# Fifty-seven passes without a use in TensorE's list, at eight places of the opening and the end

## The chip, the cores and the metric

The kernel runs on one core of one Trainium2 chip. The time is device microseconds from start to end of one execution; of the kernel before, three executions are shown by their median. One further execution was taken by the hardware profiler, and all rows below are of that one. The engines are PE (TensorE; PEld are its weight loads), DVE (VectorE), ACT (ScalarE), POOL (GpSimd) and SP (SyncE), each with its own list of instructions that it works off in order.

## The reference

For 32 batches of `x` (512 channels by 1024 nodes) a graph attention layer and a graph convolution follow each other, each with a residual and a layer norm over the last axis:

```python
q = einsum('c,bcn->bn', wq, x);  k = einsum('c,bcn->bn', wk, x)
scores = q[:, None, :] + k[:, :, None]
att = softmax(where(scores > 0, scores, 0.01 * scores), axis=-1)
agg = einsum('bcn,bmn->bcm', x, att)
x = layernorm(x + relu(einsum('oc,bcm->bom', adj, agg) + bm[None, :, None]))
W = adj * adj
x = layernorm(x + einsum('bnf,nm->bmf', x, W) + bias)
```

## The kernel before

The softmax over a sum `q + k` is not computed as a 1024 by 1024 matrix. Each batch goes through these steps, which carry short names in the order that the code writes out by hand:

- `p0` to `p27` (`project`, L329): the product of the transposed `adj` with `x`, in a form with seven instead of eight block products, into PSUM tiles `zp_A`, `zp_B`, `zp_C`. `k...` (`keep`, L348 on DVE or L350 on ACT) read them into `zrow`; `x...` (`mix`, L318) make the operands' sums.
- `qb` and `mx` (L367, L374): transposes that spread `q` and its largest value; `mx` needs `pk` (L355, DVE), and `mr` reads it.
- `r...` (`place`, L394, DVE) count each node's rank, `sd...` (`send`, L406, POOL) scatter the rows by rank to a table in DRAM, `fe` (`fetch`, L452 and L457) brings the sorted rows back as `zs`.
- `wx` (L467, ACT) and `wb` (L479, L487, DVE) make the weights `lq`; `t0` to `t8` (`table`, L501, PE) form prefix and suffix sums block by block, into a PSUM tile `tp`; `e0` to `e8` (`table_out`, L513, ACT) copy it out, `cp` (POOL) and `ca` (ACT), both L519, carry one row on to the next blocks; `ts` stores them. So t(k+1) needs e(k), then cp(k) and ca(k).
- `c...` (L419, ACT) count signs, `pi...` (`pick`, L534, POOL) gather three rows for each node. `oa`, `ox`, `no` (L549 to L566) make the mixing weights, `sc` (L573, ACT) and `ga`, `gb` (L578, DVE) mix the rows.
- `u0` to `u3` (`turn`, L587, PE) transpose the mixed rows; `ad` (L594, DVE) adds `x`; `sq` (L603), `rt` (POOL) and `y0` to `y3` (L619, ACT) are the first norm.
- `sA`, `sB` (`seed`, L649) put the bias into PSUM by two bf16 products each; `T1` to `T4` (`less`, L643, DVE) form operand differences; `m0` to `m13` (`multiply`, L666) are the second layer in seven block products, into `oA`, `oB`, `oC`. One f32 product of the program is two rows of the trace. `rd...` (L687 DVE, L689 ACT) read them, and `st`, `ro`, `sf`, `av`, `so` are the last norm and the store.

PSUM is given out by four tags, `A`, `B`, `C` and `T`, of one tile of 128 by 1024 f32 each. `bank(tag, ...)` takes the tag's tile anew, and the first write of a new tile waits until the reads of the one before are done. `T` serves `qb` of most batches and `t0` to `t7`; `t8`, `mx` and `u` use `C` in most batches.

No scheduler orders the work. `BEGIN`, `SLOT` and `END` are lists of step names, and each engine runs its instructions in the order in which the steps stand there. `BEGIN` interleaves the first batches by hand (`@b` names the batch from there on), `SLOT` is one round of the steady part, run with four batches in flight, and `END` is the drain of batches 28 to 31. The tile `first` (bf16, 128 by 1920), made once at the start, holds the smallest normal number in one corner and zeros elsewhere; `r...` uses it as a mask.

Of the kernel before, what the change touches and what calls it, by code (L numbers as in the profile page):

```python
# [23 lines left out]
def gat_gcn_resnorm_kernel(  # L24
# [823 lines left out]
    qw2 p25 @1 x04 @0 p24 k112 k011 k122 qb p26 ql p27 r0 p13 k121 r1 p12 k111 r2 en pk sd1 r3 mx @1
    p2 @0 sd0 r4 @1 p5 @0 sd3 r5 @1 p3 @0 mr sd4 r6 @1 p4 p0 @0 sd5 r7 @1 k0p1 p1 @0 sd2 @1 p7 k011
    p6 @0 sd6 @1 x14 @2 x01 @1 p12 k0u2 @0 sd7 sb0 @1 p13 p10 k0p5 p8 p9 x13 p11 k012 @2 x02 @1 p16  # L850
    @0 fe @1 k022 p17 @0 sb1 @1 p14 k1p5 p15 @0 sb2 @1 p21 k021 p19 @0 c0 @1 p18 p20 k1p1 @0 c1 @1
    k111 p22 p23 @0 wx0 wb0 t0 @2 x11 @1 k1u2 @2 x12 @1 p25 @2 x03 @0 e0 @1 p24 k112 @0 ca0 ts0 cp0
    c2 t1 @1 k122 @0 wx1 @1 qb @0 wb1 e1 @1 p27 @0 ts1 @1 ql @0 cp1 @1 pk @0 c3 @1 p26 r0 @2 p4 @1
    k121 r1 @0 c4 @1 en @0 ca1 t2 @1 r4 @0 c5 @1 sd1 r5 @2 p5 @0 e2 ca2 @1 mx @0 ts2 cp2 @1 mr @0 c6
    @1 sd4 @0 t3 @1 r2 @2 p2 @1 sd0 r3 @0 e3 ca3 ts3 cp3 @1 r6 @0 t4 @2 p1 @1 sd5 r7 @0 e4 ca4 cp4
    @1 sd3 @0 t5 @2 p3 @1 sd7 @0 e5 ts5 @2 k0p1 @0 cp5 ca5 @1 sd2 @0 t6 @2 p0 @0 e6 @2 k0p5 @0 cp6
    ts6 @2 k011 @0 ca6 @1 sd6 @0 t7 @2 x13 x14 p6 @0 e7 @2 p7 @0 ca7 cp7 ts7 t8 ts4 @2 k0u2 p11 @0
    e8 c7 @2 p10 @0 ts8 @1 fe @0 sh @2 k022 x04 p14 @0 qw3 pi0 @2 p15 p9 @1 wx0 wb0 @2 k021 @1 c0 @2
    p18 @1 t0 c1 @2 p19 @1 c2 @2 p8 @1 e0 ca0 cp0 ts0 @2 k012 @1 c3 @0 pi2 @2 k1p1 @0 pi1 @2 p22 @0
    pi3 @2 p23 @0 pi7 @2 p17 @0 pi5 @2 k1u2 p16 @1 c4 @0 pi6 @1 t1 @2 k1p5 @1 wx1 @0 pi4 @2 p24 @1  # L860
    wb1 c5 @2 p20 p12 p25 p21 p13 @0 oa0 ox0 sx no0 @2 k122 @0 sc0 @2 k112 @1 e1 @2 p27 @0 ga0 sc2
    @1 ts1 ca1 cp1 @0 sc1 gb0 @1 t2 @0 ga1 gb1 @1 e2 @0 sc3 @2 k111 @1 cp2 ca2 @0 ga2 @1 t3 @0 ga3
    gb3 @2 p26 @0 oa1 @1 e3 @0 ox1 @1 cp3 @0 no1 gb2 sc4 sc5 ga4 sc6 ga5 @1 ca3 @0 ga6 sc7 @1 t4 @0
    gb5 @1 c6 @0 ga7 gb4 gb7 @1 e4 @0 gb6 u0 @1 ca4 ts4 @2 k121 @1 cp4 ts3 c7 @0 ad0 @1 t5 ts2 @0 u1
    @1 sh e5 @0 sq0 u2 @1 cp5 @0 ad1 @1 ca5 t6 @0 rt0 @3 ld0 @2 en @0 ad2 sq1 @2 pk @0 u3 @1 e6 @3
    ld1 @2 mx @1 ca6 cp6 @0 sB @2 mr @0 sq2 rt1 ad3 @1 t7 @0 qw5 @3 ld2 @1 e7 @0 sA @1 ts6 @0 rt2 y0
    @2 qb @1 ts5 cp7 ca7 @2 r0 @1 ts7 t8 @0 sq3 @2 r1 @1 e8 @0 rt3 y1 m1 @1 ts8 @2 r2 sd1 @3 ld3 @2
    ql r3 sd0 @0 y2 m0 @2 r4 sd2 @0 y3 m7 qw4 @2 c0 @1 pi3 @0 T1 m6 @2 c1 r5 @1 pi2 @0 rdp1 m2 @1
    pi1 @0 T2 @2 c2 r6 @1 pi0 @0 m5 @2 c3 @0 T3 m4 T4 @3 x01 @0 m3 @2 r7 @0 rdu2 rd11 m9 @2 sd7 @0
    rdp5 @1 sx @2 c4 sd5 @0 m8 @1 pi5 @0 m11 rd22 @2 sd4 @0 m10 @1 pi6 oa0 ox0 @2 c5 @1 no0 @2 sd3  # L870
    @0 m13 @3 x02 @1 sc2 @3 x03 @1 sc1 @2 sd6 @0 rd12 @1 sc0 @0 m12 @3 x04 @1 pi7 @0 rd21 @1 pi4 @2
# [15 lines left out]
    r2 sd1 @29 sq3 @31 r3 sd0 @29 y1 m0 @30 pi3 @31 r4 c0 @30 pi2 @31 r5 @29 m1 @30 pi0 @29 T1 rt3
    @31 r6 @29 m2 rt2 @31 r7 sd2 @29 y2 m3 @31 sd3 @30 sx @29 rdp5 @30 pi1 @29 y3 m11 @31 sd5 @29
    rdp1 T2 @31 c1 sd7 @29 m5 @31 c2 sd6 @29 m7 @31 c3 sd4 @29 m10 @30 pi7 pi5 @29 m6 @30 oa0 ox0
    no0 @29 m4 T3 @30 sc3 sc0 @29 rd11 @31 fe @29 rdu2 T4 @31 c4 @29 m9 @30 sc2 @31 c5 @29 m8 @31 c6  # L890
    @29 rd22 @30 sc1 @31 c7 @29 rd12 m13 st0 @31 wx0 wb0 t0 @30 ga3 ga0 ga1 @31 e0 ca0 @29 st1 @31
    ts0 cp0 @30 pi6 @31 t1 @30 gb1 @29 m12 @31 e1 @30 gb3 @31 ca1 ts1 cp1 wx1 @29 ro0 @31 wb1 @29
    rd21 @31 t2 @30 pi4 ga2 @29 sf0 st2 @31 e2 ca2 cp2 t3 e3 ca3 cp3 @29 av0 ro1 @31 t4 @29 sf1 @30
    gb0 @31 e4 cp4 @30 oa1 ox1 @31 ca4 t5 @30 no1 gb2 sc4 sc5 ga4 sc7 ga5 @31 e5 @30 ga7 sc6 @31 cp5
    ca5 @30 ga6 @31 t6 @29 av1 @30 gb4 gb6 @29 so1 @30 gb5 @31 e6 @30 gb7 u1 @31 ca6 ts6 @29 st3 @31
    cp6 @29 ro2 @31 ts4 t7 ts2 @30 u0 @31 e7 ts3 ca7 @30 u3 @31 cp7 ts7 t8 @30 ad0 @31 ts5 e8 @30
    ad1 sq0 @31 ts8 @30 u2 @29 sf2 @31 sh @29 so0 @30 sq1 rt0 ad2 @31 sx @30 ad3 sq2 @31 pi0 @30 sA
    y0 rt1 @31 pi1 @30 y1 m1 @31 pi3 @30 sq3 T1 @31 pi2 @30 m0 rt2 sB rdp1 rt3 m3 y2 @31 pi7 @30 y3
    m7 @31 pi5 @30 T2 m6 @31 pi4 @30 T4 @31 pi6 @30 T3 m4 @29 ro3 @31 oa0 @30 m5 @31 ox0 no0 @30
    rd11 @31 sc2 @30 m2 rdu2 @31 ga2 sc3 @30 m9 @31 gb2 sc1 sc0 ga1 @30 rdp5 m8 @31 ga3 ga0 @29 av2  # L900
    @31 gb3 @30 m11 rd22 @31 gb0 @30 m13 @31 oa1 ox1 no1 @30 m12 @31 gb1 sc4 sc7 ga4 @30 m10 @31 sc5
    ga7 @30 rd21 @31 gb4 gb7 sc6 ga5 ga6 gb5 gb6 u0 @30 rd12 @31 u1 ad0 u2 sq0 ad1 u3 ad2 sq1 rt0
    ad3 sB y0 rt1 @30 st0 @31 sA y1 m0 @29 sf3 @31 sq2 @30 ro0 @31 T1 m1 sq3 rt2 m3 y2 rt3 y3 m2
    rdp1 T2 m6 rdp5 @30 st1 @29 av3 @31 m5 @30 sf0 st2 ro1 @31 m4 T4 @30 ro2 @31 T3 m7 rdu2 @30 sf1
    @31 rh110 @30 av1 st3 @31 m8 @30 so1 sf2 @29 so2 @30 ro3 av2 @29 so3 @31 m9 rh220 @30 av0 @31
    rh111 hb21 m10 rh221 @30 sf3 @31 hb31 @30 av3 @31 m11 rh120 @30 so3 @31 st0 @30 so0 so2 @31 m12
# [59 lines left out]
```

## Time and profile before

| | |
|---|---|
| median of three executions | 2204.18 us (2203.93 to 2204.54) |
| the profiled execution | 2203.48 us, of which the span from first to last instruction is 2201.8 us |
| mean granted TensorE clock | 0.989 |
| PE busy | 2109.1 us (96%) |
| DVE, ACT, POOL busy | 1776.1, 1653.9, 986.5 us |
| PE's longest waits in all | tp for POOL's copy, 16.6 us in 23 times; oA for ACT's y, 5.9 us in 5 times |

A row of the timeline has its start (us from the span's start), its length, the engine, the line, what is written from what, the shape, the number of instructions merged, and in brackets the idle time of that engine just ahead of it with what ended it. The busy time by stretches gives each engine's busy time in a stretch of the span, and the granted clock: 1.00 is the full clock, 0.50 half of it. Ends of PE's rows are modelled: a row outlasts the start of the next one where they are pipelined.

### The profile page before, as it was taken

To read this page: it belongs to the slowest core of one execution; us is meant where nothing else is said; L and a number is where in the kernel's file an instruction comes from. 1 tells how busy PE (TensorE), PEld (TensorE's weight loads), DVE (VectorE), ACT (ScalarE), POOL (GpSimd) and SP (SyncE) were. 2 spreads that over 40 slices of the span, in tenths; PEclk is the share of its full clock that TensorE was granted. 3 is DMA by queue.
4 is the path that set the end of the run, shared out by engine and by line. 5 is a ranking of instruction groups with operands and counts; after the bars stand their busy time and mean duration, and the time that the engine had idled before them with its cause. 6 is when DMAs were issued, how large, how long until landed. Compare 5 with 4: busy or idle time off the path is not lost.

```text
span 2201.8 us, 35460 instructions
## 1 busy us (share of the span) xinstructions
PE 2109.1 (96%) x11697; PEld 1235.6 (56%) x11697; DVE 1776.1 (81%) x3576; ACT 1653.9 (75%) x2758; POOL 986.5 (45%) x1291
## 2 busy tenths in 40 slices
...
PEclk9989999999999999999999999999999999999998
...
GB/s 249 162 224 255 263 272 280 260 236 244 263 257 280 251 240 256 262 260 280 259 244 239 270 255 282 264 244 245 263 256 279 278 247 238 260 264 270 220 206 96
DMA packets 178768, 548.84 MB, mean 249 GB/s; under 512 B 27020, under 2 KB 27032, under 8 KB 178584
## 3 DMA queue, kind: packets, MB, share of 16 engines
...
q14 instruction: 91, 0.75, 0.1%
q10 hardware_dynamic: 24, 0.01, 0.0%
...
## 4 chain that ended last, share of the span: by engine, by line
PE 73%; ACT 8%; DMA 5%; issue 4%; DVE 4%; POOL 4%; SPq 1%; POOLq 0%; DVEq 0%; ACTq 0%
PE zp_A L329 17%; PE oA L666 15%; PE tp L501 12%; PE zp_B L329 7%; PE oB L666 7%; PE op L587 5%; PE zp_C L329 4%; PE oC L666 4%; DMA zs<-td 3%; ACT rows L573 1%; ACT y L619 1%; DMA td<-zrow,ranki 1%; ACT v L689 1%; POOL zs L519 1%; PE qb L367 1%
## 5 line engine op out<-in xcount | busy, mean ns | idle before, releaser
L578 DVE SCALAR_TENSOR_TENSOR rows<-rows,ra 128x512 f32<-128x512 f32 x512 | 365.7, 738 | 19.5 <-ACT rows L573 15.7
L501 PE MATMUL tp<-zs,lq 128*64 128x257 f32 x2304 | 338.3, 394 | 27.3 <-POOL zs L519 16.6
L406 POOL DMA_INDIRECT td<-zrow,ranki x256 | 268.3, 1048 | 213.7 <-DVE idx L430 80.2
L666 PE MATMUL oA<-y,adj_sb 128*128 128x512 f32 x768 | 352.2, 601 | 9.8 <-ACT y L619 5.9
L534 POOL DMA_INDIRECT rows<-td,idx x256 | 297.2, 1161 | 90.2 <-issue 68.7
L394 DVE SCALAR_TENSOR_TENSOR junk<-qb,zrow,first 128x1024 int8<-128x1024 f32 x240 | 307.0, 1279 | 10.9 <-PE qb L367 4.0
L519 POOL COPY zs<-ts 1x513 f32<-1x513 f32 x128 | 92.0, 719 | 477.9 <-ACT ts L513 477.7
L329 PE MATMUL zp_A<-wb,x 128*64 128x257 f32 (+1 forms) x1536 | 280.3, 388 | 13.9 <-ACT v L689 6.5
L419 ACT ACTIVATE junk<-lq,kc 128x1024 int8<-128x1024 f32 x240 | 274.5, 1144 | 2.0
L594 DVE SCALAR_TENSOR_TENSOR y<-op,nbm,x 128x1024 f32<-128x1024 f32 x128 | 163.8, 1282 | 128.8 <-PE op L587 128.6
L666 PEld LDWEIGHTS oA<-y,adj_sb 128*128 128x128 f32 x768 | 146.5, 192 | 189.0 <-issue 139.5
L501 PEld LDWEIGHTS tp<-zs,lq 128*64 128x64 f32 x2304 | 171.1, 137 | 135.1 <-POOL zs L519 37.0
L573 ACT ACTIVATE rows<-rows,ra 128x512 f32<-128x512 f32 x256 | 180.0, 718 | 80.0 <-DVE ra L566 78.4
L329 PEld LDWEIGHTS zp_A<-wb,x 128*64 128x64 f32 (+1 forms) x1536 | 178.6, 155 | 77.4 <-ACT v L689 17.8
L350 ACT COPY zrow<-zp_A 128x514 f32<-128x514 f32 x192 | 112.7, 587 | 143.6 <-PE zp_A L329 129.8
L519 POOL COPY zs<-zs 1x513 f32<-1x513 f32 x128 | 79.0, 617 | 253.3 <-ACT zs L513 253.3
L619 ACT ACTIVATE y<-y,nb,r 128x1024 f32<-128x1024 f32 x128 | 158.8, 1241 | 4.3
L695 DVE BATCH_NORM_STATS2 st<-v 128x6 f32<-128x512 f32 x240 | 151.8, 674 | 0.0
L603 ACT ACTIVATE x<-y,nm 128x1024 f32<-128x1024 f32 x128 | 147.2, 1150 | 4.2
L719 ACT ACTIVATE v<-v,nb,rs 128x1024 f32<-128x1024 f32 x120 | 148.1, 1234 | 2.3 <-DVE nb L711 1.4
L587 PE MATMUL op<-ident,rows 128*128 128x128 f32 x1024 | 141.5, 283 | 4.2 <-DVE rows L578 2.0
L587 PEld LDWEIGHTS op<-ident,rows 128*128 128x128 f32 x1024 | 114.9, 143 | 46.0 <-issue 24.6
...
## 6 DMA issues: line engine op xcount, KB each, us to landing
x<-in_x_dram SPq DMA_DIRECT2D x128, 512.0 KB, 4.5
out_dram<-v SPq DMA_DIRECT2D x120, 512.0 KB, 2.9
...
td<-ts SPq DMA_DIRECT2D x224, 120.2 KB, 2.0
...
```

Source lines behind the costliest of these rows:

```text
L329: nc.tensor.matmul(zp[n : n + wide, m, 0:CE], side(b, g, a)[:, c, m * P + n : m * P + n + wide], wb[:, w, c, :], start=first and c == 0, s ...
L394: nc.vector.scalar_tensor_tensor(junk(b)[:, 0:N], qbs[b], zrow[:, nt, 0:1], first[:, o : o + N], ALU.subtract, ALU.is_lt, accum_out=rank[: ...
L406: sc = nc.gpsimd.indirect_dma_start(out=td[:, :], out_offset=bass.IndirectOffsetOnAxis(ap=ranki[:, nt : nt + 1], axis=0), in_=zrow[:, nt, ...
L419: nc.scalar.activation(junk(b)[:, N : 2 * N], qs[b], AF.Sign, bias=kcs[b][:, nt : nt + 1], accum_out=signs(b)[:, nt : nt + 1],)
L501: nc.tensor.matmul(tp[i * G : (i + 1) * G, h, 0:CE], lw[:, ks[i], :], zs[:, j, 1 + h * CE : 1 + (h + 1) * CE], start=True, stop=True,)
L519: copy(zs[row : row + 1, to, 1:ZW], ts[row : row + 1, 0 : ZW - 1])
L534: nc.gpsimd.indirect_dma_start(out=rows[:, mt, :], out_offset=None, in_=tdb[b % 2].rearrange("(s u) c -> s (u c)", u=3), in_offset=bass.In ...
L573: nc.scalar.activation(u, u, AF.Copy, scale=ratios(b)[:, k, 1:2])
L578: nc.vector.scalar_tensor_tensor(u, rg[:, k, i, 1 : C + 1], ratios(b)[:, k, i : i + 1], u, ALU.mult, ALU.add)
L587: nc.tensor.transpose(op[:, mt * P : (mt + 1) * P], rg[:, mt, 1, 1 + ot * P : 1 + (ot + 1) * P], ident)
L619: nc.scalar.activation(yall[:, ot], yall[:, ot], AF.Identity, bias=nb, scale=r)
L666: nc.tensor.matmul(o[:, m, :], quarters[w][:, a, m * P : (m + 1) * P], part(b, y)[:, a, :], start=fresh and a == 0, stop=a == CT // 2 - 1, ...
```

## The change

A new helper takes a PSUM tag's tile and writes its first half with n bf16 products of 128 by 128 with 128 by 512, each a write of its own, none of them read by anything:

```diff
+    def stay_warm(b, tag, n):
+
+        idle = bank(tag, [P, N], f"idle_{tag}_{nc.next_id()}")
+        for i in range(n):
+            nc.tensor.matmul(idle[:, lo], first[:, 0:P], first[:, 0:H], start=True, stop=True)
...
+    also(0, "wC3", stay_warm, "C", 3)
+    also(0, "wC6", stay_warm, "C", 6)
+    also(0, "wT10", stay_warm, "T", 10)
+    also(0, "wT11", stay_warm, "T", 11)
+    also(0, "wT4", stay_warm, "T", 4)
+    also(0, "wT5", stay_warm, "T", 5)
+    also(0, "wT8", stay_warm, "T", 8)
```

The seven names stand at eight places in the lists, three in `BEGIN` and five in `END`; the rest of both lists is as it was (the diff rewraps their lines). The lines that hold them:

```diff
     BEGIN
+    qw2 p25 @1 x04 @0 p24 k112 k011 k122 qb p26 ql p27 r0 p13 k121 r1 p12 k111 r2 en pk sd1 r3 wT10
+    mx @1 p2 @0 sd0 r4 @1 p5 @0 sd3 r5 @1 p3 @0 mr sd4 r6 @1 p4 p0 @0 sd5 r7 @1 k0p1 p1 @0 sd2 @1 p7
...
+    @0 pi3 @2 p23 @0 pi7 @2 p17 @0 pi5 @2 k1u2 p16 @1 c4 @0 pi6 @1 wT5 t1 @2 k1p5 @1 wx1 @0 pi4 @2
...
+    ga0 sc2 @1 ts1 ca1 cp1 @0 sc1 gb0 @1 wT11 t2 @0 ga1 gb1 @1 e2 @0 sc3 @2 k111 @1 cp2 ca2 @0 ga2
...
     END
+    r2 sd1 @29 sq3 @31 r3 sd0 @29 y1 wC3 m0 @30 pi3 @31 r4 c0 @30 pi2 @31 r5 @29 wC6 m1 @30 pi0 @29
...
+    ca5 @30 ga6 @31 wT8 t6 @29 av1 @30 gb4 gb6 @29 so1 @30 gb5 @31 e6 @30 gb7 u1 @31 ca6 ts6 @29 st3
...
+    pi0 @30 wT10 sA y0 rt1 @31 pi1 @30 y1 m1 @31 pi3 @30 sq3 T1 @31 pi2 @30 wT4 m0 rt2 sB rdp1 rt3
```

On PE the passes stand as follows: ten ahead of batch 0's `mx`; five ahead of batch 1's `t1`; eleven ahead of batch 1's `t2`; three ahead of batch 29's `m0` and six between its `m0` and `m1`; eight ahead of batch 31's `t6`; ten ahead of batch 30's `sA` and four between its `m1` and `m0`. That is 57 passes, each with a weight load.

More of the change, by code (lines that the diff above doesn't have):

```diff
@@ L847, in gat_gcn_resnorm_kernel @@
     k012 p14 p17 k021 p16 p18 k1p5 @1 x11 @0 p19 @1 x02 @0 qw1 p20 k1p1 p22 p23 p21 k1u2 @1 x12 @0
[L848 to L871, printed above, removed]
@@ L872, in gat_gcn_resnorm_kernel @@
-    c6 c7 @1 sc3 @2 fe
+    qw2 p25 @1 x04 @0 p24 k112 k011 k122 qb p26 ql p27 r0 p13 k121 r1 p12 k111 r2 en pk sd1 r3 wT10
+    mx @1 p2 @0 sd0 r4 @1 p5 @0 sd3 r5 @1 p3 @0 mr sd4 r6 @1 p4 p0 @0 sd5 r7 @1 k0p1 p1 @0 sd2 @1 p7
+    k011 p6 @0 sd6 @1 x14 @2 x01 @1 p12 k0u2 @0 sd7 sb0 @1 p13 p10 k0p5 p8 p9 x13 p11 k012 @2 x02 @1
+    p16 @0 fe @1 k022 p17 @0 sb1 @1 p14 k1p5 p15 @0 sb2 @1 p21 k021 p19 @0 c0 @1 p18 p20 k1p1 @0 c1
+    @1 k111 p22 p23 @0 wx0 wb0 t0 @2 x11 @1 k1u2 @2 x12 @1 p25 @2 x03 @0 e0 @1 p24 k112 @0 ca0 ts0
@@ new lines, in gat_gcn_resnorm_kernel @@
+    cp0 c2 t1 @1 k122 @0 wx1 @1 qb @0 wb1 e1 @1 p27 @0 ts1 @1 ql @0 cp1 @1 pk @0 c3 @1 p26 r0 @2 p4
+    @1 k121 r1 @0 c4 @1 en @0 ca1 t2 @1 r4 @0 c5 @1 sd1 r5 @2 p5 @0 e2 ca2 @1 mx @0 ts2 cp2 @1 mr @0
+    c6 @1 sd4 @0 t3 @1 r2 @2 p2 @1 sd0 r3 @0 e3 ca3 ts3 cp3 @1 r6 @0 t4 @2 p1 @1 sd5 r7 @0 e4 ca4
+    cp4 @1 sd3 @0 t5 @2 p3 @1 sd7 @0 e5 ts5 @2 k0p1 @0 cp5 ca5 @1 sd2 @0 t6 @2 p0 @0 e6 @2 k0p5 @0
+    cp6 ts6 @2 k011 @0 ca6 @1 sd6 @0 t7 @2 x13 x14 p6 @0 e7 @2 p7 @0 ca7 cp7 ts7 t8 ts4 @2 k0u2 p11
@@ new lines, in gat_gcn_resnorm_kernel @@
+    @0 e8 c7 @2 p10 @0 ts8 @1 fe @0 sh @2 k022 x04 p14 @0 qw3 pi0 @2 p15 p9 @1 wx0 wb0 @2 k021 @1 c0
+    @2 p18 @1 t0 c1 @2 p19 @1 c2 @2 p8 @1 e0 ca0 cp0 ts0 @2 k012 @1 c3 @0 pi2 @2 k1p1 @0 pi1 @2 p22
+    @0 pi3 @2 p23 @0 pi7 @2 p17 @0 pi5 @2 k1u2 p16 @1 c4 @0 pi6 @1 wT5 t1 @2 k1p5 @1 wx1 @0 pi4 @2
+    p24 @1 wb1 c5 @2 p20 p12 p25 p21 p13 @0 oa0 ox0 sx no0 @2 k122 @0 sc0 @2 k112 @1 e1 @2 p27 @0
+    ga0 sc2 @1 ts1 ca1 cp1 @0 sc1 gb0 @1 wT11 t2 @0 ga1 gb1 @1 e2 @0 sc3 @2 k111 @1 cp2 ca2 @0 ga2
@@ new lines, in gat_gcn_resnorm_kernel @@
+    @1 t3 @0 ga3 gb3 @2 p26 @0 oa1 @1 e3 @0 ox1 @1 cp3 @0 no1 gb2 sc4 sc5 ga4 sc6 ga5 @1 ca3 @0 ga6
+    sc7 @1 t4 @0 gb5 @1 c6 @0 ga7 gb4 gb7 @1 e4 @0 gb6 u0 @1 ca4 ts4 @2 k121 @1 cp4 ts3 c7 @0 ad0 @1
+    t5 ts2 @0 u1 @1 sh e5 @0 sq0 u2 @1 cp5 @0 ad1 @1 ca5 t6 @0 rt0 @3 ld0 @2 en @0 ad2 sq1 @2 pk @0
+    u3 @1 e6 @3 ld1 @2 mx @1 ca6 cp6 @0 sB @2 mr @0 sq2 rt1 ad3 @1 t7 @0 qw5 @3 ld2 @1 e7 @0 sA @1
+    ts6 @0 rt2 y0 @2 qb @1 ts5 cp7 ca7 @2 r0 @1 ts7 t8 @0 sq3 @2 r1 @1 e8 @0 rt3 y1 m1 @1 ts8 @2 r2
@@ L873, in gat_gcn_resnorm_kernel @@
+    sd1 @3 ld3 @2 ql r3 sd0 @0 y2 m0 @2 r4 sd2 @0 y3 m7 qw4 @2 c0 @1 pi3 @0 T1 m6 @2 c1 r5 @1 pi2 @0
+    rdp1 m2 @1 pi1 @0 T2 @2 c2 r6 @1 pi0 @0 m5 @2 c3 @0 T3 m4 T4 @3 x01 @0 m3 @2 r7 @0 rdu2 rd11 m9
+    @2 sd7 @0 rdp5 @1 sx @2 c4 sd5 @0 m8 @1 pi5 @0 m11 rd22 @2 sd4 @0 m10 @1 pi6 oa0 ox0 @2 c5 @1
+    no0 @2 sd3 @0 m13 @3 x02 @1 sc2 @3 x03 @1 sc1 @2 sd6 @0 rd12 @1 sc0 @0 m12 @3 x04 @1 pi7 @0 rd21
+    @1 pi4 @2 c6 c7 @1 sc3 @2 fe
     """
@@ L886, in gat_gcn_resnorm_kernel @@
     @30 t8 @31 ql r0 @29 rt1 @31 p26 @30 e8 @31 r1 @29 sB @30 ts8 @31 k121 @29 y0 @31 en @29 sA @31
[L887 to L906, printed above, removed]
@@ L907, in gat_gcn_resnorm_kernel @@
-    rh121 ro0 st1 m13 rh210 sf0 hb20 ro1 av0 sf1 ag2 rh211 so0 ro2 av1 hb30 ag3 sf2 ro3 fa21 so1
-    fa20 fo20 sf3 fa31 fa30 fo21 fo31 fo30
+    r2 sd1 @29 sq3 @31 r3 sd0 @29 y1 wC3 m0 @30 pi3 @31 r4 c0 @30 pi2 @31 r5 @29 wC6 m1 @30 pi0 @29
+    T1 rt3 @31 r6 @29 m2 rt2 @31 r7 sd2 @29 y2 m3 @31 sd3 @30 sx @29 rdp5 @30 pi1 @29 y3 m11 @31 sd5
+    @29 rdp1 T2 @31 c1 sd7 @29 m5 @31 c2 sd6 @29 m7 @31 c3 sd4 @29 m10 @30 pi7 pi5 @29 m6 @30 oa0
+    ox0 no0 @29 m4 T3 @30 sc3 sc0 @29 rd11 @31 fe @29 rdu2 T4 @31 c4 @29 m9 @30 sc2 @31 c5 @29 m8
@@ new lines, in gat_gcn_resnorm_kernel @@
+    @31 c6 @29 rd22 @30 sc1 @31 c7 @29 rd12 m13 st0 @31 wx0 wb0 t0 @30 ga3 ga0 ga1 @31 e0 ca0 @29
+    st1 @31 ts0 cp0 @30 pi6 @31 t1 @30 gb1 @29 m12 @31 e1 @30 gb3 @31 ca1 ts1 cp1 wx1 @29 ro0 @31
+    wb1 @29 rd21 @31 t2 @30 pi4 ga2 @29 sf0 st2 @31 e2 ca2 cp2 t3 e3 ca3 cp3 @29 av0 ro1 @31 t4 @29
+    sf1 @30 gb0 @31 e4 cp4 @30 oa1 ox1 @31 ca4 t5 @30 no1 gb2 sc4 sc5 ga4 sc7 ga5 @31 e5 @30 ga7 sc6
+    @31 cp5 ca5 @30 ga6 @31 wT8 t6 @29 av1 @30 gb4 gb6 @29 so1 @30 gb5 @31 e6 @30 gb7 u1 @31 ca6 ts6
@@ new lines, in gat_gcn_resnorm_kernel @@
+    @29 st3 @31 cp6 @29 ro2 @31 ts4 t7 ts2 @30 u0 @31 e7 ts3 ca7 @30 u3 @31 cp7 ts7 t8 @30 ad0 @31
+    ts5 e8 @30 ad1 sq0 @31 ts8 @30 u2 @29 sf2 @31 sh @29 so0 @30 sq1 rt0 ad2 @31 sx @30 ad3 sq2 @31
+    pi0 @30 wT10 sA y0 rt1 @31 pi1 @30 y1 m1 @31 pi3 @30 sq3 T1 @31 pi2 @30 wT4 m0 rt2 sB rdp1 rt3
+    m3 y2 @31 pi7 @30 y3 m7 @31 pi5 @30 T2 m6 @31 pi4 @30 T4 @31 pi6 @30 T3 m4 @29 ro3 @31 oa0 @30
+    m5 @31 ox0 no0 @30 rd11 @31 sc2 @30 m2 rdu2 @31 ga2 sc3 @30 m9 @31 gb2 sc1 sc0 ga1 @30 rdp5 m8
@@ new lines, in gat_gcn_resnorm_kernel @@
+    @31 ga3 ga0 @29 av2 @31 gb3 @30 m11 rd22 @31 gb0 @30 m13 @31 oa1 ox1 no1 @30 m12 @31 gb1 sc4 sc7
+    ga4 @30 m10 @31 sc5 ga7 @30 rd21 @31 gb4 gb7 sc6 ga5 ga6 gb5 gb6 u0 @30 rd12 @31 u1 ad0 u2 sq0
+    ad1 u3 ad2 sq1 rt0 ad3 sB y0 rt1 @30 st0 @31 sA y1 m0 @29 sf3 @31 sq2 @30 ro0 @31 T1 m1 sq3 rt2
+    m3 y2 rt3 y3 m2 rdp1 T2 m6 rdp5 @30 st1 @29 av3 @31 m5 @30 sf0 st2 ro1 @31 m4 T4 @30 ro2 @31 T3
+    m7 rdu2 @30 sf1 @31 rh110 @30 av1 st3 @31 m8 @30 so1 sf2 @29 so2 @30 ro3 av2 @29 so3 @31 m9
```

3 lines of the change are left out of this document (added).

## The prediction

> **What bounds the kernel now.** The first view is the page: PE is busy 96% of the span, and its granted clock is whole in nearly every slice.
>
> ```profile
> span 2201.8 us, 35460 instructions
> PE 2109.1 (96%) x11697; PEld 1235.6 (56%) x11697; DVE 1776.1 (81%) x3576; ACT 1653.9 (75%) x2758; POOL 986.5 (45%) x1291
> PEclk9989999999999999999999999999999999999998
> ```
>
> The slices that fall short lie in the first 160 us and the last 160 us, where the eight edits are. The second view is busy time by stretches, cut where the clock changes. Columns: stretch, length, busy us of PE, PEld, DVE, ACT, POOL (instructions in brackets), clock, DMA share, GB/s.
>
> ```profile
> 42.11:45.52 3.41, 0.82 (x9) 0.32 (x5) 3.33 (x10) 0.00 (x0) 0.00 (x0) 1.00 0.00 0
> 45.52:48.93 3.41, 3.41 (x9) 2.76 (x10) 3.34 (x6) 0.00 (x0) 3.04 (x2) 0.50 0.22 82
> ...
> 106.96:110.37 3.41, 1.55 (x14) 1.06 (x16) 0.57 (x2) 2.71 (x6) 0.00 (x0) 1.00 1.06 208
> ...
> 127.44:130.85 3.41, 1.60 (x12) 0.76 (x8) 2.97 (x5) 2.90 (x5) 1.41 (x2) 1.00 0.97 395
> 130.85:134.27 3.42, 2.88 (x10) 1.96 (x11) 3.09 (x8) 1.29 (x3) 0.48 (x1) 0.50 0.05 17
> ```
> ```profile
> 2055.97:2059.38 3.41, 1.59 (x4) 0.30 (x2) 3.29 (x8) 3.31 (x7) 1.53 (x2) 1.00 0.19 60
> ...
> 2090.11:2093.52 3.41, 1.64 (x9) 0.67 (x8) 3.38 (x9) 1.57 (x4) 0.28 (x1) 1.00 0.68 136
> ...
> 2107.17:2110.58 3.41, 0.97 (x7) 0.57 (x7) 3.17 (x5) 3.36 (x6) 0.82 (x1) 1.00 0.00 0
> 2110.58:2114.00 3.42, 3.42 (x17) 2.13 (x15) 3.42 (x6) 1.94 (x3) 1.53 (x3) 0.50 0.53 179
> ...
> 2120.82:2124.24 3.42, 0.75 (x5) 0.21 (x3) 2.50 (x4) 3.36 (x10) 1.67 (x3) 1.00 0.60 216
> 2124.24:2127.65 3.41, 1.88 (x3) 0.79 (x3) 0.31 (x1) 3.31 (x8) 2.78 (x5) 0.50 0.69 224
> ```
>
> What to see: a stretch in which PE is busy 1.60 us or less is followed by one at half clock; 1.55 and 1.64 were not. A half-clock stretch with 2.88 us busy stays at half; one with 3.36 or more (141.09 to 144.51) goes back. So half clock stands at 45.52 (one stretch), 130.85 (four), 2059.38 (two), 2110.58 (one), 2124.24 (two), 2158.37 (one): 37.5 us, of which at most half, 18.8 us, is to be had back.
>
> The third view is PE's timeline and the chain that ended last, to see which of those stretches set the end.
>
> ```profile
> 126.74 1.09 PE L329 MATMUL zp_A<-wb,x 128*64 128x257 f32 x8 [1.25 <-DVE zrow L348]
> 128.46 1.22 PE L501 MATMUL tp<-zs,lq 128*64 128x257 f32 x8 [0.63 <-POOL zs L519]
> 131.38 2.25 PE L501 MATMUL tp<-zs,lq 128*64 128x257 f32 x8 [1.71 <-POOL zs L519]
> ```
> ```profile
> 2057.44 1.13 PE L666 MATMUL oA<-y,adj_sb 128*128 128x512 f32 x2 [1.00 <-ACT y L619]
> 2060.26 5.49 PE L666 MATMUL oA<-y,adj_sb 128*128 128x512 f32 x6 [1.70 <-ACT y L619]
> ...
> 2091.18 1.31 PE L501 MATMUL tp<-zs,lq 128*64 128x257 f32 x8 [0.74 <-DVE lq L479]
> 2093.89 1.09 PE L501 MATMUL tp<-zs,lq 128*64 128x257 f32 x8 [1.40 <-POOL zs L519]
> ...
> 2109.72 1.92 PE L501 MATMUL tp<-zs,lq 128*64 128x257 f32 x8 [2.44 <-POOL zs L519]
> ...
> 2125.90 6.25 PE L666 MATMUL oA<-y,adj_sb 128*128 128x512 f32 x8 [1.53 <-ACT y L619]
> ```
>
> PE waits here for others: between t0 (2091.18) and t6 (2109.72) the chain goes round through PE tp, ACT copy L513, POOL copy L519 and the next tp, so whatever delays one table step delays all that follow.
>
> **The passes' price.** The nearest row is the seed, the same bf16 128x512 form: 128 of them, median 378 ns each, the second of a pair 0.215 us after the first. So a pass takes 0.215 us of PE, 0.43 at half clock, and 57 take 12.3 us at full clock. Their weight loads (95 to 101 ns in the seed's rows) hide behind them. No other engine gets or loses an instruction, and none of their orders changes. New waits are PE's alone: t1, t2 and t6 now also wait for the last pass to have left bank T (378 less 215 ns, 0.16 us).
>
> **Opening.** *wT10* before mx: PE is idle 2.59 us to 45.49, ten passes take 2.15 and fit. The stretch at 42.11 rises to 3.0 us busy, and half clock at 45.52 goes: PE is 1.7 us ahead. It gives this back at the first t0 (68.92), which stands behind DVE's lq (68.53 to 69.10) and that behind a fetch. Worth 0. *wT5* before t1: no gap is there; t1 starts at 118.88 under the products before it. Its 1.07 us push PE's work from 125.48 to 126.55, and the product at 126.74 waits for DVE anyhow. Costs 0; the cover is that 1.25 us. *wT11* before t2 must wait until ACT has read bank T (e1, 126.71 to 127.28) and then takes 2.36 us, to about 130.1, where the gap before t2 is 0.63: t2 is 1.7 late. Queued behind it: e2 on ACT, the scales after it, cp2 on POOL, t3. In return the stretch 127.44 is full, and t3 takes 1.1 instead of 2.25, so e3 is 0.55 late, and with it the weights of the second half and the gains on DVE. The stretch 134.27 holds only the one product (1.0 us), so half clock comes at 137.68 and stays to 144.51 as before. t5 begins 0.55 late, ends partly in the full clock: +0.35 at e5, from which ACT is without a pause to 157.3, where PE waits for its y. Opening: +0.35 us.
>
> **End.** *wC3* before m0 takes 0.65 of a gap of 1.00: no cost, and the stretch 2055.97 rises to 2.2. *wC6* stands after m0. But the 1.70 us wait is inside m0: its first product (two rows) runs at 2057.44, the second needs y1 at 2060.26. So its six passes (1.29) fill no wait of before; they lie in front of m2's wait for T1 (DVE to 2063.83) and push m2 about 0.3 past it. Still, 2059.38 to 2066.21 at full clock brings m3's end from 2069.49 to about 2067.6; the read after it waits for ACT's y2 and gains 1.2. All later products of batch 29 come 1.2 earlier, and the last of them ends at 2089.3, not 2090.44. That brings nothing: t0 stands behind lq, that behind the exponent at 2090.36, and that behind the fetch by DMA, whose sends are in a POOL queue without a pause from 2057.54.
>
> It costs something. The stretch from 2090.11 held 1.64 us: 0.33 of that last product and t0's 1.31. With 1.31 alone it is under every value that kept the clock, and half clock comes at 2093.52. t1 takes 1.98 (the row of t4 at 138.33) for 1.09: +0.9. The product after it takes 3.4 instead of 1.7 if the half clock lasts. t2, behind both, is 1 to 2 late. I take +1.5.
>
> *wT8* before t6 waits for ACT's e5 (to 2108.78), then takes 1.72, so t6 starts at 2110.7 rather than 2109.72: +1.0. If the stretch then holds over 1.6 (1.8 if t5 stands where it did), t6 and the transposes after it are at full clock: t6 ends +0.1, the first transpose group waits for DVE's last gain, and the chain is 0.25 ahead at t7. If it began at half clock, the passes take 3.4 and t6 is 2.7 late. Between these, with t2 late by 1.5, I take +0.7. *wT10* before sA: 2.15 in a gap of 2.67, no cost, stretch 2120.82 up to 2.9, full clock at 2124.24. m1's second product then waits for y1 (ACT, 2127.31). *wT4* stands after m1, again not in a wait: 0.86 on the path. m0 ends at 2130.8 for 2132.15: -1.4, with which ACT's read, y2, y3 and all PE's products to 2152 move. But at full clock 2124.24 holds barely 1.3 to 1.6, so half clock may come at 2127.65, and then nothing is won. I take -1.0. 2158.37 is untouched.
>
> Sum: 0.35 + 1.5 + 0.7 - 1.0 = +1.55 us on the profiled execution's 2203.48, which is 0.70 under the median: 2204.18 + 1.55 = about 2205.7.
>
> [...] Rows: every drop above follows gaps of at most 2.69 us. [...]
>
> **Rivals.** *Only the gains:* no new drop at 2093.52: 0.35 - 0.25 - 1.4 = -1.3, 2202.9; for it, 1.55 once kept the clock; against it, t0 alone is 1.31. *Half clock stays in the table steps (slower):* they fill 1.1 of each 2.5 us, at half clock 2.0 of 3.4, and 2.88 did not bring the clock back. From t1 on: 0.9, the product behind it 1.1, t5 0.9, wT8 2.7, no gain at wT4: with the opening about +6, 2210. It decides as soon as two of the stretches from 2090 to 2110 hold under 1.55. [...] *All is won:* half clock off the chain at t3 to t5 (2.4), t6 and transposes (1.7), m1 and m0 (2.6), less about 1.7 of delay: -5, 2199.2; against it, the short stretches at 134.27 and 2124.24.
>
> **How the numbers follow.** A measurement of this kernel tells 0.2%, 4.4 us, from no change. Likeliest, a small loss, 2203.5 to 2209: 0.35. Only gains: 0.18. Half clock stays: 0.27. Not counted: 0.08, its price on the bound, so half to each side. All won: 0.12. With 0.03 of the likeliest beyond the bound: faster 0.12, same 0.32 + 0.18 + 0.04 = 0.54, slower 0.27 + 0.04 + 0.03 = 0.34. The range reaches down past the gains to 2201 and up to the lasting half clock, 2210.5.
>
> **What would show it.** Right: clock 1.00 at 45.52 and 2059.38 to 2066; t2 of the opening about 1.7 later against e1; the last product of batch 29 ended over a microsecond before t0, and clock 0.50 from about 2093; t6 begun behind the passes. Wrong: half clock right after full passes (not counted); t0 earlier against e8 of the batch before (then PE did set it); a half clock in the steady part, where PE is never idle long; or the opening ahead rather than behind when PE closes its gaps at 157.

## The result, and the profile after

The changed kernel took 2208.53 us (median of 15 runs) beside 2203.57 us for the kernel before: ratio 1.0032, 95% interval 1.0023 to 1.0042, so 5 to 9 us slower (the two medians alone differ by 4.96 us, the lower end of that). Timed again later (c4 below) it gave 1.0009 (0.9998 to 1.0020). The forecast, +1.55 us and most likely no change that can be told, is near the second; the first is a clear loss, and needs the experiments.

The page of the changed kernel, the lines that answer to those of before:

```profile
span 2212.2 us, 35540 instructions
PE 2120.4 (96%) x11718; PEld 1239.5 (56%) x11754; DVE 1777.0 (80%) x3576; ACT 1655.3 (75%) x2758; POOL 985.2 (45%) x1291
PEclk9999999999999999999999999999999999999988
```

The profiled execution took 2213.86 us and is the second slowest of the 15, so the profile shows about twice the loss of the median. PE has 11.3 us more busy time, about what 57 passes were to take (12.3). The 8 in the third slice of the clock row of before is gone: half clock stands for 30.7 us ahead of the tail, where before had 37.5. So the passes kept some of the clock, and yet the span is 10.4 us longer. In the later timing it is the same: c4 has a mean granted clock of 0.9917 against 0.9899 for before, so 0.0018 x 2203 us, about 4 us, less is lost to the clock, and it is not faster.

Where the time went is read by setting the n-th instruction of VectorE (it has as many in both kernels, in one order) against its twin in the profile of before. The shift is -0.6 us at 100 us, +3.2 at 160, wanders between -0.1 and +4.8 in the steady part, is +4.5 at 2040 and +10.4 at 2180. So 3.8 us came in the opening and 5.8 in the end. Of the 5.8, 2.4 is batch 31's t0 behind its fetch, 1.8 lies in the table steps between t0 and t6, 2.2 at t6, 0.9 after 2160, and the products of batch 29 give 1.4 back.

PE's timeline in the opening:

```profile
115.11 1.96 PE L329 MATMUL zp_A<-wb,v 128*64 128x257 f32 x16 [1.43 <-ACT zrow L350]
116.90 1.91 PE L329 MATMUL zp_B<-wb,v 128*64 128x257 f32 x16
118.96 1.03 PE L754 MATMUL idle_T<-first 128*128 128x512 bf16 x4 [0.16 <-issue]
123.62 1.09 PE L501 MATMUL tp<-zs,lq 128*64 128x257 f32 x8 [3.63 <-issue]
...
130.10 1.04 PE L329 MATMUL zp_A<-wb,x 128*64 128x257 f32 x8
131.07 2.55 PE L754 MATMUL idle_T<-first 128*128 128x512 bf16 x10
133.72 1.09 PE L501 MATMUL tp<-zs,lq 128*64 128x257 f32 x8
136.20 1.68 PE L501 MATMUL tp<-zs,lq 128*64 128x257 f32 x8 [1.38 <-POOL zs L519]
```

t1 (the first tp) begins at 123.62, where it stood at 118.88. It is 4.7 us late (5.0 against the work before it, which is 0.25 early), and not the 1.07 us of five passes; the row says "issue": it waited for nothing that the profile shows. (One record of each group of passes is missing here.) Because t1 is late, PE goes without a gap to 131.07, and wT11 (eleven passes, 2.55) lies in front of t2 in full.

Busy time by stretches in the end, cut every 3.41 us (the clock changes of this profile, at 2098.04, 2104.87, 2111.70 and 2121.93, fall on these borders; columns as before: PE, PEld, DVE, ACT, POOL, clock, DMA share, GB/s):

```profile
2094.63:2098.04 3.41, 1.36 (x8) 0.72 (x8) 1.76 (x4) 0.67 (x2) 0.00 (x0) 1.00 0.81 193
2098.04:2101.45 3.41, 2.06 (x9) 0.92 (x9) 3.38 (x7) 1.24 (x3) 1.62 (x2) 0.50 0.46 118
...
2108.28:2111.70 3.42, 1.36 (x12) 0.57 (x8) 0.90 (x3) 2.96 (x4) 1.38 (x3) 1.00 0.06 25
2111.70:2115.11 3.41, 2.63 (x8) 1.04 (x8) 2.85 (x9) 2.45 (x6) 0.60 (x1) 0.50 0.01 2
2115.11:2118.52 3.41, 2.46 (x6) 0.94 (x7) 3.10 (x5) 3.36 (x5) 0.75 (x1) 0.50 0.00 0
2118.52:2121.93 3.41, 3.26 (x12) 1.22 (x11) 2.98 (x6) 0.09 (x2) 0.00 (x0) 0.50 0.38 154
```
```profile
2096.63 1.36 PE L501 MATMUL tp<-zs,lq 128*64 128x257 f32 x8 [3.06 <-DVE lq L479]
2099.39 1.98 PE L501 MATMUL tp<-zs,lq 128*64 128x257 f32 x8 [1.40 <-POOL zs L519]
2101.30 3.74 PE L666 MATMUL oA<-y,adj_sb 128*128 128x512 f32 x4
...
2116.09 0.58 PE L754 MATMUL idle_T<-first 128*128 128x512 bf16 x1 [0.73 <-ACT zs L513]
2116.90 2.76 PE L754 MATMUL idle_T<-first 128*128 128x512 bf16 x6 [0.22 <-issue]
2119.81 1.98 PE L501 MATMUL tp<-zs,lq 128*64 128x257 f32 x8
```

With t0 alone in it (1.36 us) the stretch at 2094.63 is followed by half clock, as the prediction said; t1 takes 1.98 and the product behind it 3.74. A second drop follows the stretch at 2108.28, again 1.36. The passes of wT8 then run in a half-clock stretch: 2.76 us for six, against 0.215 each at full clock. t6 begins only at 2119.81, and with it the whole chain. The stretch at 2118.52 gets to 3.26 us with 1.1 us of passes in it, and the clock is back at 2121.93; without them it would have held 2.1 (3.26 less 1.1), and 2.06, 2.46 and 2.63 brought nothing back. So the passes weighed in here, though what they read is nearly zero, and the "not counted" of the forecast, given 0.08, is out. (All the columns of `first` that the passes read hold the smallest normal number; its zeros lie further right, past column 895.)

### The profile page after: what moved, and what is told of

Same layout as the page of the kernel before. It is cut to its first block, busy times and chain, and to the rows that moved or that the text cites. A ratio compares the mean times of both kernels' runs of the same rounds, so it can differ in the third digit from the quotient of the medians.

```text
span 2212.2 us, 35540 instructions
## 1 busy us (share of the span) xinstructions
PE 2120.4 (96%) x11718; PEld 1239.5 (56%) x11754; DVE 1777.0 (80%) x3576; ACT 1655.3 (75%) x2758; POOL 985.2 (45%) x1291
## 4 chain that ended last, share of the span: by engine, by line
PE 67%; DMA 8%; ACT 7%; DVE 7%; issue 6%; POOL 4%; SPq 1%; DVEq 0%; POOLq 0%; ACTq 0%
PE zp_A L329 16%; PE oA L666 12%; PE tp L501 11%; PE zp_B L329 8%; PE op L587 5%; PE oB L666 5%; DMA zs<-td 4%; PE zp_C L329 4%; PE oC L666 3%; DMA td<-zrow,ranki 2%; DVE junk L394 2%; POOL rows L534 1%; ACT rows L573 1%; ACT y L619 1%; POOL zs L519 1%
```

## The experiments

Fifteen kernels ran, those of one letter on one chip, each letter on a chip of its own. Ratios are to the kernel before on the same chip; a gain or cost given as "measured" is the ratio in us. For the reading I use the shift of VectorE's instructions in the profile of each against the first profile of before, across four places: the opening (from 100 to 160 us), batch 29's products (2064 to 2085), t6 (2109 to 2115.5), and batch 30's m1 and m0 (2115.5 to 2140). Negative is time gained. The last column says which groups the kernel holds.

```
             ratio (95%)              opening  prod.29    t6    m1/m0   passes
after        1.0032 (1.0023-1.0042)    +3.77   -1.42   +2.23   +0.01   all
a1_open      1.0018 (1.0008-1.0028)    +5.20   -1.31   +0.83   +0.20   wT10 wT5 wT11 (opening)
a2_m29       0.9997 (0.9986-1.0007)    -0.71   +0.02   -0.20   +0.53   wC3 wC6
a3_t6        0.9996 (0.9986-1.0005)    -0.89   -1.42   +1.34   +0.36   wT8
a4_m30       0.9995 (0.9985-1.0005)    -1.49   -1.41   -0.19   -1.08   wT10 wT4 (end)
b1_w5        0.9991 (0.9982-1.0000)    -1.00   -1.43   -0.23   -0.42   wT5
b2_w11       1.0004 (0.9994-1.0015)    +1.83   -1.41   +0.04   -0.25   wT11
b3_end       0.9997 (0.9986-1.0008)    -0.55   -1.42   -0.32   -1.08   the five of the end
b4_w10       0.9993 (0.9984-1.0002)    -0.39   -1.31   -0.19   -1.08   wT10 (opening)
c1_w5_w11    1.0007 (0.9993-1.0022)    +0.95   -1.41   -0.22   -0.40   wT5 wT11
c2_no_w5     1.0008 (0.9996-1.0021)    +0.53   -1.42   -0.34   -1.09   all but wT5
c3_no_w11    1.0000 (0.9985-1.0015)    -0.54   -1.42   -0.34   -1.09   all but wT11
c4_all       1.0009 (0.9998-1.0020)    +1.75   -1.42   -0.34   -0.09   all
d1_waits     1.0021 (1.0006-1.0036)    -1.38   +0.01   +0.02   -1.08   all but wT11, wT8
d2_w15_w11   1.0018 (1.0008-1.0028)    +5.63   -1.42   -0.20   -1.13   fifteen for wT5, wT11
d3_w15       1.0000 (0.9991-1.0010)    +2.92   -1.40   -0.20   +0.53   fifteen for wT5
```

The columns are single executions: kernels that hold the same passes at a place differ there by up to 1.3 us. In the steady part between them, which the passes do not touch, the shift wanders by 4 to 7 us in every kernel, so whole spans are not compared.

**One place at a time (a1 to a4).** Each kernel keeps the groups of one place and leaves the others out. For a3, against the kernel before:

```diff
-    ca5 @30 ga6 @31 t6 @29 av1
+    ca5 @30 ga6 @31 wT8 t6 @29 av1
```

> Only the three groups of the opening (ten before batch 0's mx, five before t1, eleven before t2 of batch 1). Theory (passes ahead of a table step stand on the path whenever TensorE comes to them late): in the profile after, t1 waited for its fetch to 123.6 us and TensorE then had no pause to 131.07, so all eleven passes, 2.6 us, lay in front of t2; expected +1 to +3 us against the kernel before, and the steady part late by as much. Rival (the sum of the prediction): +0.35 us. Second rival (the loss of the whole change is only the spread of the fetches): 0.

> Only the three and the six passes at batch 29's m0. Theory (TensorE, faster, ends batch 29's products earlier, waits longer before t0 and loses its clock there): products at full clock after 2059, but clock 0.50 from the stretch after t0 of batch 31, t1 1.98 us for 1.09, the product behind it 3.4 to 3.7 for 1.9, t2 late by 1.5 to 2 against t0; +1.5 to +2.5 us. Rival (the two stretches won at full clock shorten the end): -1 to -3 us. Rival (nothing there is on the path): 0.

> Only the eight passes before batch 31's t6. Theory (their price hangs on the clock that they meet): here they run at full clock, 0.215 us each, t6 starts 1.0 us later but runs at full clock: t7 ahead by 0.3, in all -0.5 to +0.5 us; in the whole change they ran at half clock and t6 was 2.3 late. Rival (bare cost): +1.0 us or more.

> Only the ten passes before batch 30's sA and the four between its m1 and m0. Theory: the ten fit their gap; m1 runs at full clock, but the wait for y1 then leaves the stretch under 1.6 us of work and half clock comes one stretch later, so 0 to -1.5 us. Rival (full clock through both): -1.4 to -2. Rival (bare cost of the four): +0.9.

Measured: the opening's three cost +4.0 us (1.8 to 6.2), more than the +1 to +3 expected; the end's parts -0.7, -0.9 and -1.1, none of them told from nothing. Two of the profiles show what a group costs when it meets half clock. In a2 (first fence) a half-clock stretch covers 2061.07 to 2064.49, and the six passes of wC6 take 2.59 us between the two halves of the products; in b3 (second) the same group at full clock takes 1.46:

```profile
2060.68 1.72 PE L666 MATMUL oA<-y,adj_sb 128*128 128x512 f32 x2 [1.70 <-ACT y L619]
2062.20 2.59 PE L754 MATMUL idle_C<-first 128*128 128x512 bf16 x6
2064.62 1.88 PE L666 MATMUL oA<-y,adj_sb 128*128 128x512 f32 x4
```
```profile
2060.06 1.13 PE L666 MATMUL oA<-y,adj_sb 128*128 128x512 f32 x2 [1.70 <-ACT y L619]
2061.03 1.46 PE L754 MATMUL idle_C<-first 128*128 128x512 bf16 x6
2062.32 1.88 PE L666 MATMUL oA<-y,adj_sb 128*128 128x512 f32 x4
```

The third column of the table holds the consequence: a2 and d1, whose wC6 meets half clock, gain nothing on before. The other five kernels with these groups gain 1.42, and the nine without them gain 1.31 to 1.43. So the gain that the prediction gave to wC3 and wC6 is there without them: the profile of before, with two half-clock stretches in that place, was the exception. Nor is it half clock alone that a2 and d1 pay for: a1, a4 and b4 have one half-clock stretch in the same products, no pass, and the gain of 1.31 to 1.41. The passes bring nothing at full clock and cost 1.3 us at half clock.

wT8 is the same. In a3 it falls into the half clock of 2105.67 to 2115.91, and t6 waits for it:

```profile
2109.04 2.06 PE L501 MATMUL tp<-zs,lq 128*64 128x257 f32 x8 [1.42 <-POOL zs L519]
2112.13 3.57 PE L754 MATMUL idle_T<-first 128*128 128x512 bf16 x8 [1.04 <-ACT zs L513]
2115.85 1.10 PE L501 MATMUL tp<-zs,lq 128*64 128x257 f32 x8
```

b1, which has no wT8 and half clock from 2102.66 to 2112.89, goes from t5 to t6 directly:

```profile
2105.73 2.06 PE L501 MATMUL tp<-zs,lq 128*64 128x257 f32 x8 [1.42 <-POOL zs L519]
2109.72 2.36 PE L501 MATMUL tp<-zs,lq 128*64 128x257 f32 x8 [1.92 <-POOL zs L519]
```

From t5 to t6 it is 6.81 us in a3 and 3.99 in b1. In the t6 column that is +2.23 (changed kernel) and +1.34 (a3) where wT8 meets half clock, and -0.32 to -0.34 (b3, c2, c3, c4) where it does not; without wT8 it is -0.23 to +0.04 in nine of ten kernels, and +0.83 in a1, whose half clock lasts from 2104.58 to 2118.23.

**The opening split, and the end as a whole (b1 to b4).** b1, b2 and b4 keep one group of the opening, b3 the five of the end. For b2:

```diff
-    ga0 sc2 @1 ts1 ca1 cp1 @0 sc1 gb0 @1 t2 @0 ga1
+    ga0 sc2 @1 ts1 ca1 cp1 @0 sc1 gb0 @1 wT11 t2 @0 ga1
```

> Only wT5 is kept (five passes in front of t1 of batch 1, all other passes left out). The four groups were tried in parts before: the opening's three cost +4.0 us (1.8 to 6.2), the end's parts nothing or a little gain. Theory 1 (the passes of wT11 alone make the cost, since they stand in front of t2 whatever came before): this kernel within 1 us of before, ratio 0.9996 to 1.0004. Theory 2 (each of wT5 and wT11 would fall into a gap of its own, and only both together are longer than the gaps): also within 1 us, and wT11 alone likewise. Theory 3 (wT5 itself is the cost: in both profiles that hold it the signal that ends its five passes comes 2.15 us after the products' signal, twice the 1.07 us of five passes at full clock, and t1 and the products behind it wait for it): +2 to +4 us, ratio 1.0009 to 1.0018. In its trace: the start of t1 against the 118.88 us of before.

> Only wT11 is kept (eleven passes in front of t2 of batch 1). Theory 1 (wT11 alone is the cost): the passes last 2.4 us, 0.63 us of it is the gap that t2 had in front of it, so t2 is 1.8 us later, and nothing of it comes back in the following table steps, which wait for ScalarE and GpSimd and not for the clock: +1.5 to +3 us, ratio 1.0007 to 1.0014. Theory 2 (only both together): +0.35 us as forecast, the half clock of t3 to t5 being saved, ratio within 0.9996 to 1.0005. Theory 3 (wT5 is the cost): within 0.5 us.

> All five groups of the end are kept (wC3, wC6, wT8, and wT10 and wT4 before the products of batch 30), the three of the opening left out. The parts one by one gave -0.9, -0.9 and -1.2 us (each with about 2 us of uncertainty). If they add: -2.7 us, ratio 0.9988. If they meet (the passes of batch 29 move t0 of batch 31 such that half clock is granted through t1 and on to wT8, whose passes then take 0.43 us each and hold t6 back, as in the profile of the changed kernel): +2 to +4 us, ratio 1.0009 to 1.0018, and then this and the opening's +4.0 make the +7 of the whole change. If the opening is all there is: within 1 us.

> Only the opening's wT10 is kept (ten passes behind the products of batch 0, at 45 us of the profile). By all theories it costs nothing: the engine waits there, and what it gains, the half clock of 45.5 to 48.9 us, is in a stretch in which TensorE waits for others. Within 1 us, ratio 0.9996 to 1.0004. If it is here that the opening loses its 4 us: 1.0010 or more.

Measured: -2.0 us (-4.0 to 0), +0.9 (-1.3 to +3.3), -0.7 (-3.1 to +1.8), -1.5 (-3.5 to +0.4). That wT5 is the cost is out. So is the expectation that the end's groups cost 2 to 4 us together: they do so in single executions, not in the median. In the trace of b2, wT11 alone puts t2 3.68 us behind the product of x in front of it, where before had 1.72 (126.74 to 128.46): t2 is 2.0 us late, and the steady part begins at +1.83.

```profile
125.70 1.09 PE L329 MATMUL zp_A<-wb,x 128*64 128x257 f32 x8 [1.55 <-DVE zrow L348]
126.72 2.55 PE L754 MATMUL idle_T<-first 128*128 128x512 bf16 x11
129.38 1.09 PE L501 MATMUL tp<-zs,lq 128*64 128x257 f32 x8
```

**The pair, and the whole without one (c1 to c4).** c1 keeps wT5 and wT11; c2 and c3 are the changed kernel without the one or the other; c4 is the changed kernel.

```diff
-    @0 gb0 @1 wT11 t2 @0 ga1
+    @0 gb0 @1 t2 @0 ga1
```
The cut is that of c3, against the changed kernel.

> Only wT5 and wT11 are kept, the two groups in front of t1 and t2 of batch 1. The opening's three together had cost +4.0 us (1.8 to 6.2), each alone -2.0, +0.9 and -1.5 us (each with about 2 us of uncertainty). Theory 1 (the two share one gap: the 1.25 us before the products of x takes wT5's delay alone, and 0.63 us before t2 is all that wT11 finds; together wT5's delay uses the gap up and wT11 is then paid in full): +2 to +4 us, ratio 1.0009 to 1.0018, and t2 over 3 us late in the trace. Theory 2 (they add, each as alone): -1 us, ratio 0.9995, and t2 1.8 us late. Theory 3 (the +4.0 belonged to the chip of that call: its four profiles all show products of batch 1 that end 0.3 to 1.8 us later than their rows, those of the other call none): -1 us here unless this chip shows it too.

> The changed kernel without wT5, all other groups kept. Theory 1 (the two share one gap): the opening's cost falls to that of wT11 alone, so this is about 4 us below the changed kernel timed beside it, ratio to before about 1.001. Theory 2 (all add as alone: opening -0.6 without wT5, end -0.7): ratio 0.9994. Were the changed kernel's cost in the end alone: no different from the changed kernel.

> The changed kernel without wT11, all other groups kept. Theory 1 (the two share one gap, and of the two wT11 is what is paid): the opening costs nothing, so 5 to 7 us below the changed kernel timed beside it, ratio to before 0.9985 to 1.0000. Theory 2 (all add as alone): ratio 0.9981, likewise below. Were wT5 the cost: no different from the changed kernel.

> The changed kernel as it is, on the same chip as the three beside it, for what they are compared with. Its first timing gave 1.0032 (1.0023 to 1.0042). If its cost is in the program: again 1.002 to 1.004. If a good part belonged to the chip of that timing (theory 3): 1.000 to 1.0015.

Measured: +1.5 us (-1.5 to +4.8), +1.8 (-0.9 to +4.6), 0.0 (-3.3 to +3.3), +2.0 (-0.4 to +4.4). The intervals are too wide to tell the four apart; the traces do better. c4 in the opening:

```profile
118.33 1.03 PE L754 MATMUL idle_T<-first 128*128 128x512 bf16 x4 [0.16 <-issue]
119.46 1.09 PE L501 MATMUL tp<-zs,lq 128*64 128x257 f32 x8
...
125.94 1.04 PE L329 MATMUL zp_A<-wb,x 128*64 128x257 f32 x8
126.91 2.55 PE L754 MATMUL idle_T<-first 128*128 128x512 bf16 x10
129.56 1.09 PE L501 MATMUL tp<-zs,lq 128*64 128x257 f32 x8
```

Here t1 comes right behind the passes, as forecast, and the product of x at 125.94 stands where it would without wT5 (126.74 before, all work of this profile being 0.9 earlier): its cost is covered by the 1.25 us gap. Sort the opening column by what the kernels hold, and it falls into groups: without wT11, and t1 at most 2 us late, -0.39 to -1.49 (eight kernels, mean -0.87), with wT5 or without; with wT11 and such a t1, +0.53 to +1.83 (b2, c1, c2, c4, mean +1.27), with wT5 or without. wT11 costs 2.1 us, and wT5 nothing. The two do not share a gap; theory 1 of c1 falls.

The timings, taken together, say the same of wT11. All seven kernels that hold it are slower than before (1.0004 to 1.0032); of the nine without it, eight stand at 0.9991 to 1.0000, and only d1 (below) at 1.0021. On the chips of b and c, the kernels with wT11 are 1.8 to 2.3 us above those without; on the chip of a, a1 is 4.9 us above the others (it holds wT5 and wT10 too, and there t1 comes late); on the chip of d, d2 is 4.0 above d3 but 0.7 below d1.

**A late t1 on purpose (d2, d3), and the groups in real gaps (d1).** In the changed kernel's first profile and in a1 t1 was late by 5 and 3.5 us. The semaphore events of these traces say how. In a1 PE's event at the end of the products before the passes comes at 118.19, though their rows end at 117.12, and the event at the end of the five passes at 120.35, though their rows end at 118.30. ScalarE's copy that waits for the same products shows it in the changed kernel, 2.56 us behind the row's end (118.81):

```profile
121.37 0.59 ACT L350 COPY zrow<-zp_B 128x514 f32<-128x514 f32 x1 [2.53 <-issue]
```

In the median an event stands 0.015 us behind the end of its row. All four profiles of the chip that ran a1 to a4 have such a lag in this place (0.3 to 1.8 us, in products that stand before the place of the passes), that of before and those of the two chips that ran b and c have none. The three profiles of the chip of d have it too. So in eight profiles, the changed kernel's among them, the products are known as done only late here, and other engines wait for that. Whether it belongs to the chips is not shown: in these same eight, 56 to 74 of PE's completions have no event of their own in the trace, in the nine others none, so how these executions were recorded may play a part. In a1 the gap before t1 also cost the clock: the stretch up to 121.43 held 1.27 us, half clock follows, and the two rows of products behind t1 take 1.88 and 1.99 us for 1.07. d2 and d3 make t1 late by other means, with and without wT11:

```diff
-    also(0, "wT5", stay_warm, "T", 5)
+    also(0, "wT5", stay_warm, "T", 15)
```

> The changed kernel without wT11 and without wT8: what is left are the groups that stood in real gaps of TensorE in the profiles (wT10 and wT5 of the opening, wC3, wC6, and wT10 and wT4 of the end). If the groups' costs are as read from the traces (wT11 +0.9 us at t3, wT8 up to 2.3 us where it meets half clock, the others 0 or a gain): 1 to 3 us faster than before, ratio 0.9985 to 0.9995. If the gains seen in single profiles were the place of the gate's stretches in those executions and not the passes: 0.9995 to 1.0003.

> The pair wT5 and wT11, with fifteen passes instead of five in front of t1, so that t1 comes 2.15 us later still, as it did by other means in the two profiles that lost 3 us here. Theory 1 (a late t1 uses up the 1.25 us gap, and wT11 is then paid in full at t2): t2 over 3.5 us late, the steady part begins about 3 us late, ratio 1.0010 to 1.0020. Theory 2 (t1 is not what counts, something else on that chip was): as with five passes, the steady part 0.1 to 0.9 us late, ratio 1.0000 to 1.0008.

> Fifteen passes in front of t1 of batch 1 and nothing else. Theory 1: t1 is 3.4 us late, of which the gap before the products of x takes 1.25 us and the one before t2 0.63 us, so t2 is about 1.5 us late; ratio 1.0003 to 1.0010. Theory 2 (t1 has more cover than these two gaps): t2 on time, ratio within 0.9995 to 1.0003.

PE's timeline of d2:

```profile
117.79 3.41 PE L754 MATMUL idle_T<-first 128*128 128x512 bf16 x15
122.66 1.09 PE L501 MATMUL tp<-zs,lq 128*64 128x257 f32 x8 [1.46 <-issue]
...
129.14 1.04 PE L329 MATMUL zp_A<-wb,x 128*64 128x257 f32 x8
130.11 2.55 PE L754 MATMUL idle_T<-first 128*128 128x512 bf16 x11
132.76 1.09 PE L501 MATMUL tp<-zs,lq 128*64 128x257 f32 x8
```

t1 is 5 us late, and d2 loses +4.0 us (1.8 to 6.2), as much as a1; its opening is +5.63, like a1's +5.20 and the changed kernel's +3.77. d3, without wT11, is at 0.0 us (-2.0 to +2.2), with +2.92 in its profile. From d3 to d2 wT11 costs 3.2 us between the medians and 2.7 in the profiles. So a t1 that is 5 us late costs up to 3.8 us in the trace (+2.92 against -0.87), though d3's timing shows none of it, and wT11 its 2 to 3 us on top. That a late t1 with wT11 makes a loss like a1's, 4 us, is shown. That it made the 5 to 9 us of the changed kernel is argued: its one profile has it, but what its other runs had is not known.

d1 went against its expectation: 1.0021, slower by 1 to 8 us, though its profile has nothing that costs (opening -1.38, t6 +0.02, m1 and m0 -1.08). Its parts had measured -0.7 to -2.0 one by one. That profile, at 2200.00 us, is the fastest of d1's 12 runs, whose median is 2204.86, so it need not show what the others paid; the medians of d1 and of before differ by only 2.45 us. I have no cause for it. As d1 without wT11 lost as much as d2, the timings on this chip do not show wT11's cost by themselves; the traces do. It says at least that the groups which stand in real gaps gain nothing to speak of, and that an interval from one timing may be narrower than the truth: so says also c4 beside the first timing, the same kernel, whose intervals do not meet. No version was found that beats the kernel before.

## Why the prediction was wrong, point by point

- **wT11, "+0.35 us".** The delay was right: t2 1.7 us late was forecast, 1.9 to 2.0 measured against the product in front of it in b2, c1, c2 and c4. The return was not. It was to come from a t3 at full clock and from half clock that "stays to 144.51 as before". Before, in the one profile, had four half-clock stretches there; the eight other profiles without wT11 or a very late t1 all have two between 127 and 146 us, four of them with no pass in the opening at all. With wT11, b2, c1, c2 and c4 have two as well, from 137.06 to 139.66 on, where the prediction put them. So the step "in return" credited the passes with what other executions have for nothing: the term is +2.1 us beside executions without wT11 (+1.27 against -0.87), where +0.35 was put.
- **wT5, "costs 0; the cover is 1.25 us".** Right as long as t1 is late by what five passes take: b1, c1, c3 and c4 show it. The cover is gone when PE's own products end late, as in a1 and in the changed kernel's profile. The profile of before has no such lag, so nothing in it could warn; the step had no range of its own, and the prediction's range was built from the end's terms.
- **wC3 and wC6, +1.5 by way of half clock at 2093.52.** The chain came as described (t0 alone in its stretch, t1 at 1.98, the product at 3.74), but it is not these groups that bring it. From 2093 to 2109 the seven kernels with them lose 1.03 us in the mean, the nine without 0.98. The five that lose 1.8 to 2.2 us (changed kernel, a3, c3, c4, d3) are those in which t0 itself came 1.3 to 2.4 us late behind its fetch; a3 and d3 hold no such group. A late t0 leaves the stretch empty. The gain of 1.2 in the products before is no work of the passes either.
- **wT8, "+0.7".** A mean between two cases that do not mix: -0.1 at full clock, 1.3 to 2.2 at half clock. (Over the six kernels that hold it the mean is +0.37, against -0.05 in the ten without.) The bound named beside it (t6 2.7 late, if half clock had begun) was the right one for the profiled execution.
- **wT10 and wT4 of the end, "-1.0".** Got in five of seven kernels that hold them (-1.08), not in the changed kernel and c4, where half clock lay on m1. But b4 and d2 have -1.08 and -1.13 without them. Means: -0.79 with, -0.18 without; so the term is about -0.6, from few executions.
- **wT10 of the opening, "0".** Right: b4's opening is -0.39, inside the group without passes.
- **The rivals.** "Not counted" is out, by the stretch at 2118.52; its price, which the chances put on the bound, no run shows. "Half clock stays in the table steps" describes the end of the changed kernel's profile, with the loss at t1, behind it, and at wT8; these are 4.0 of the 5.8 us there, and not the rule: b3, which holds all groups of the end, has -0.7 us.
- **The sum.** With the measured terms, 2.1 (wT11), -0.6 (m1 and m0) and somewhere between 0 and 2 for wT8 and wC6 when they meet half clock, it is +1.5 to +3.5. c4's +2.0 fits this. That the rest of the first timing's 5 to 9 us is the late t1 was not shown; it stays open.

Behind most of these stands one error: gains were read off one profile of before, whose half clock lay in worse places than in most others. Half clock did not stand at one place in every execution: at the first gap it begins at 45.52 in the profile of before, at 44.42 in b1, at 47.44 in a3, and is absent in a2, b2, d2 and d3; none of these holds a pass there. (All seven kernels with wT10 in the opening lack it, so the passes do work; they are only not needed each time.) A change that fills one stretch cannot count on the stretch.
